# Source lists of a sparse graph network: which operand of the list products moves

## The chip, the cores and the metric

The kernel runs on one core of a Trainium2 chip. The time is that of the device for one execution, in microseconds, as the median of several runs. Beside these runs there is one profiled execution, from which all durations come. The engines are TensorE (PE, with its weight loads as PEld), VectorE (DVE), ScalarE (ACT), GpSimd (POOL) and SyncE (SP, a queue of DMAs).

## The reference

Four graph attention layers run one after the other over 4096 nodes of 256 features, all with the same 0/1 adjacency matrix of 4096 x 4096 (about one entry in 256 is set, many more for the first nodes than for the last). Each layer normalises its input, applies ReLU, and adds its attention to the input:

```python
h = jnp.maximum(_layernorm(x, axis=-1), 0.0)
x = x + layer(h, adj, ...)
# in a layer, in short:
h = x @ W
e = leaky_relu((h @ a1)[:, None] + (h @ a2)[None, :])
attn = softmax(where(adj > 0, e, NEG), axis=1)
out = attn @ h            # layer 2 has 4 heads, layer 3 a positive and a negative softmax
```

## The kernel before

**Dense blocks and listed tiles.** Targets are handled in 8 blocks of 512 or in 32 row tiles of 128. The first blocks of each layer are dense (4 in layer 0, then 2, 1, 1): all 32 source tiles are weighed and multiplied. For the other row tiles the sources beyond the first 512 nodes are listed. Since few sources have an edge into a tile, each tile T has CAPS[T] columns (5 to 12) of 128 source numbers each. A column serves either one quarter of the tile's 32 targets (a quad is four such columns) or the whole tile. GpSimd gathers feature rows by these numbers with indirect DMAs (L532).

**How a list is made.** The lists are made once, during layer 0, by `list_sources(ib, ...)` for the blocks 1 to 7, 28 row tiles in all. VectorE finds from the mask which sources each quarter sees. Two products with triangular and all-ones matrices, `pre` (L864) and `tot` (L866), and a scan give every used source a place. The place is split in a column number (`hib`) and a row within the column (`lof`). `val` holds for each column the source's number where it belongs to that column, and else 0. `one_hot` (L943) makes `first[p, i, j]`, which is 1 where source p of source tile j has row i; one such tile is for 14 of the 28 source tiles, and j is its innermost index, so the 128 entries of one j lie 28 bytes apart. Then, for each row tile, 28 products, one for each source tile j, add up the list (L968): the one-hot is the weights, and val moves, CAPS[T] columns of it. The result is `idx_ps`, 128 rows by CAPS[T] columns; VectorE adds an offset and writes it as the integers `idx` (L978), which the gathers read.

**The order of work.** `run(plan)` writes out by hand the order in which instructions are issued. A step of the plan is one source tile of one unit (a dense block or a listed tile). Each step goes through fetch, begin, weigh (on VectorE, `s_p`, L1151, or L1110 for quads) and multiply (on TensorE, `s_acc`, L1193, or L1130 for quads, whose products are 32 columns wide), which come 0, 2, 3 and 6 steps after one another. After each multiply, `pump` gives turns to waiting generators: `posts` (ends of units and the next layer's projections, `s_tp`, L746, `s_hT`, L748, and `s_pj`, L778) and `lists_q` (the list being made). A turn runs to the generator's next `yield`. The first dense blocks and listed tiles give the list two turns a step, dense block 2 three and dense block 3 four. When layer 0's plan is over, lists and posts are drained with one turn each in alternation; layer 1 follows.

**What is shared.** TensorE, VectorE and ScalarE each work in the order of issue. The PSUM pool `ps_mm` has two buffers under the tag "mm", for the list's results and sums, `s_tp`, `s_pj` and the target rows `s_sT` (L1036). The list's `idx_ps` holds one of them from a tile's first product to `idx`. ScalarE, besides copies and exponentials, copies masks out of gathered rows (L1084, L1174), and waits for those gathers.

Of the kernel before, what the change touches and what calls it, by code (L numbers as in the profile page):

```python
# [8 lines left out]
F32 = mybir.dt.float32  # L9
F16 = mybir.dt.float16  # L10
# [4 lines left out]
ALU = mybir.AluOpType  # L15
# [3 lines left out]
P = 128  # L19
# [438 lines left out]
JT = NT - DP  # L458
# [5 lines left out]
GR = 4  # L464
GP = P // GR
# [3 lines left out]
MAXCAP = max(CAPS)  # L469
# [20 lines left out]
def list_layers(ctx: ExitStack, tc: tile.TileContext, a: dict, out: bass.AP, flag):  # L490

    nc = tc.nc

    const = ctx.enter_context(tc.tile_pool(name="s_const", bufs=1))
# [6 lines left out]
    ps_mm = ctx.enter_context(tc.tile_pool(name="s_mm", bufs=2, space=PSUM))  # L501
# [11 lines left out]
    onesb = const.tile([P, P], F16, name="s_onesb")  # L513
# [3 lines left out]
        tri, onesb, pattern=[[1, P]], compare_op=ALU.is_gt, fill=0.0, base=0, channel_multiplier=-1  # L517
    )
    nc.gpsimd.affine_select(
        tri, tri, pattern=[[1, P]], compare_op=ALU.not_equal, fill=-float(BASE), base=0, channel_multiplier=-1  # L520
    )
    places = const.tile([P, NT - TS0], F32, name="places")
    for T in range(TS0, NT):
        nc.gpsimd.memset(places[:, T - TS0 : T - TS0 + 1], float(2 * BASE + P * SHARED[T]))
# [326 lines left out]
    def list_sources(ib, seen, pool, consts):  # L851
# [3 lines left out]
        half = JT // 2  # L855
        quads = QUADS[ib * IT]
        cap = max(CAPS[ib * IT : (ib + 1) * IT])
# [68 lines left out]
        val = pool.tile([P, MAXCAP, n], F16, name=f"val_{ib}", tag="val")  # L926
# [13 lines left out]
        def one_hot(T, j):  # L940

            first = pool.tile([P, P, half], F16, name=f"first_{T}_{j}", tag="first", bufs=2)
            nc.vector.tensor_tensor(  # L943
                first,
                place,
                lof[:, T % IT, j : j + half].unsqueeze(1).to_broadcast([P, P, half]),
                op=ALU.is_equal,
            )
            return first
# [5 lines left out]
        for t in range(IT):  # L955
            T = ib * IT + t
            cap = CAPS[T]
            ps = None
            for j in range(JT):
                if j % half == 0:  # L960
                    first = firsts.pop()
                    ahead.pop(0)
                    if ahead:
                        firsts.append(one_hot(*ahead[0]))
                    yield
                if ps is None:
                    ps = ps_mm.tile([P, MAXCAP], F32, name=f"idx_ps_{T}", tag="mm")
                nc.tensor.matmul(  # L968
                    ps[:, 0:cap],
                    lhsT=first[:, :, j % half],  # L970
                    rhs=val[:, 0:cap, t * JT + j],
                    start=(j == 0),
                    stop=(j == JT - 1),
                )
                if j % 7 == 6:
                    yield
            idx = keep.tile([P, cap], I32, name=f"idx_{T}", tag=f"idx_{T}")
            nc.vector.tensor_scalar(idx, ps[:, 0:cap], float(HALF), None, op0=ALU.add)  # L978
            index[T] = idx
            yield  # L980
# [413 lines left out]
    with ExitStack() as phase:  # L1394
# [33 lines left out]
        half = CH // 2  # L1428
# [32 lines left out]
        def mask_chunk(ib, c):  # L1461
# [17 lines left out]
            if ib > 0:  # L1479
                if c == 0:  # L1480
                    seen[ib] = lists_p.tile([P, IT * GR, JT], BF16, name=f"seen_{ib}", tag="seen", bufs=4)
                else:
                    nc.vector.tensor_reduce(
                        seen[ib][:, :, (c - 1) * CH : c * CH].rearrange("p a j -> p j a"),
                        m.rearrange("p j i -> p (j i)")
                        .bitcast(I32)
                        .rearrange("p (j a w) -> p j a w", j=CH, w=GP // 4),
                        AX.X,
                        ALU.max,
                    )  # L1490
                if c == NCH - 1:
                    waiting[ib] = list_sources(ib, seen[ib], lists_p, consts)
                    while turns and turns[0] in waiting:
                        push(lists_q, waiting.pop(turns.pop(0)))
# [86 lines left out]
    for l in (1, 2, 3):  # L1581
# [37 lines left out]
        if l == 3:  # L1619
            one = Unit(L, 0, IT, NT, all_sources(L, 0, IT, [0], 1), big="growb", heads=[0])  # L1620
            two = Unit(L, 0, IT, NT, all_sources(L, 0, IT, [1], 1), big="growb", heads=[1], like=one)
            first = one.plan() + two.plan()
        else:
            per = L.H
            first = []
# [40 lines left out]
def gat_layers(tc: tile.TileContext, a: dict, out: bass.AP):  # L1666
    nc = tc.nc
    with tc.tile_pool(name="flag", bufs=1) as pool:
        flag = pool.tile([1, 1], I32, name="flag")

        with tc.manual_schedule(engines={mybir.EngineType.Pool}):
            list_layers(tc, a, out, flag)
        again = nc.values_load(flag[0:1, 0:1], min_val=0, max_val=1)
        with tc.If(again > 0):
            dense_layers(tc, a, out)
# [45 lines left out]
```

## Time and profile before

| | us |
|---|---|
| median of 3 runs | 1661.9 |
| their range | 1661.72 to 1684.04 |
| profiled execution | 1527.76 |
| its span | 1526.0 |

| in the profiled execution | |
|---|---|
| list products (L968) | 784, from 126.4 to 498.3 us |
| one-hots (L943) | 56 on VectorE, 1080 ns each |
| idx (L978) | 28, the first at 139.2, the last at 498.5 us |
| mean granted TensorE clock | 0.955 |

The page of a profile gives busy times, shares of the span and the chain of work that ended last. A product's duration includes the time that it needs to pass through the array, and products overlap, so what a product costs in a row of products is read from the distance of starts. "x <- y" after a wait means that x stood idle until y was done.

### The profile page before, as it was taken

The page shows a single profiled execution, that of the slowest core. Times are in us where ns is not written, and L with a number is a line of the kernel's source. Part 1 is how long each engine was busy: PE and PEld are TensorE (multiplying, and loading weights), DVE is VectorE, ACT ScalarE, POOL GpSimd, SP SyncE. Part 2 cuts the span into 40 slices and gives each one's busy share as a digit, 9 for nine tenths or more (in the row PEclk, how much of TensorE's full clock was granted, in tenths as well). Part 3 has the DMA queues.
Part 4 walks back from the last instruction along what each step waited for, and adds up shares of the span by engine and source line. Part 5 has one row for each costly group of instructions (what it writes and reads, how often), then busy time and mean ns, then how long its engine had stood idle before and what let it go on. Part 6 is the DMA issues. An engine that isn't in the chain of part 4 may idle for free.

```text
span 1526.0 us, 30153 instructions
## 1 busy us (share of the span) xinstructions
PE 1387.2 (91%) x10558; PEld 1051.8 (69%) x10558; DVE 1179.9 (77%) x3424; ACT 499.9 (33%) x1569; POOL 1061.1 (70%) x1255
## 2 busy tenths in 40 slices
PE   5999898989998999987898999999677999999995
PEld 4888676767776877775644655667565887878873
DVE  6979898999887478755598999999776466777764
ACT  5641012112112023332336666578662111111111
POOL 9832888888530578867608878888764588777775
PEclk9999999999998899999999999999888999999997
DMA  7899999997622455555514344345442677777665
GB/s 256 285 321 312 294 306 306 253 240 192 186 63 80 136 143 155 157 155 158 145 51 118 101 121 120 112 122 131 123 131 79 189 221 228 213 206 219 192 180 150
DMA packets 161024, 272.72 MB, mean 179 GB/s; under 512 B 29664, under 2 KB 86462, under 8 KB 160862
## 3 DMA queue, kind: packets, MB, share of 16 engines
q1 hardware_dynamic: 117322, 146.32, 30.8%
q0 software_dynamic: 42704, 123.84, 30.4%
q8 instruction: 86, 1.41, 0.4%
q14 instruction: 76, 0.62, 0.1%
q10 hardware_dynamic: 836, 0.53, 0.1%
HBM read 225.22 MB, written 45.39 MB: 177 GB/s over the span
## 4 chain that ended last, share of the span: by engine, by line
PE 52%; DVE 18%; DMA 11%; POOL 11%; issue 5%; ACT 2%; SPq 0%; POOLq 0%; DVEq 0%; ACTq 0%
PE s_acc L1193 31%; PE s_pj L778 8%; DVE s_p L1151 7%; POOL s_gq L532 5%; DMA s_gq<-table,idx 5%; DMA s_raw<-in_adjT 4%; PE s_acch L1210 3%; PE s_accm L1228 2%; PE s_acc L1130 2%; POOL s_gg L532 2%; DVE s_p L1160 2%; PE idx_ps L968 2%; PE s_tp L746 2%; POOL pause L541 1%; DVE s_m L1472 1%
## 5 line engine op out<-in xcount | busy, mean ns | idle before, releaser
L532 POOL DMA_INDIRECT s_gq<-table,idx x400 | 444.0, 1110 | 121.9 <-issue 83.1
L532 POOL DMA_INDIRECT s_gg<-table,idx x258 | 287.7, 1115 | 229.2 <-DVE bad L1015 58.5
L1193 PE MATMUL s_acc<-g,s_p 128*128 128x257 f32 x1152 | 294.8, 399 | 20.6 <-DVE s_p L1151 20.2
L1193 PEld LDWEIGHTS s_acc<-g,s_p 128*128 128x128 f32 x1152 | 219.0, 199 | 62.9 <-DVE s_p L1151 29.2
L1193 PE MATMUL s_acc<-s_gs,s_p 128*128 128x257 f32 x896 | 214.1, 390 | 0.0
L1151 DVE SCALAR_TENSOR_TENSOR s_p<-s_grow,pre,mpre 128x128 f32<-128x128 f32 (+1 forms) x576 | 188.4, 364 | 29.6 <-PE s_acc L1193 24.6
L778 PE MATMUL s_pj<-s_w,s_hT 128*128 128x259 f32 (+3 forms) x640 | 180.6, 421 | 17.5 <-ACT s_g L813 10.2
L1193 PEld LDWEIGHTS s_acc<-s_gs,s_p 128*128 128x128 f32 x896 | 167.9, 193 | 38.5 <-DVE s_p L1151 5.9
L1193 PE MATMUL s_acc<-pre,s_p 128*128 128x257 f32 x768 | 183.0, 386 | 2.3 <-DVE s_p L1151 1.5
L1151 DVE SCALAR_TENSOR_TENSOR s_p<-s_grow,s_gs,s_ms 128x512 f32<-128x512 f32 x224 | 157.7, 744 | 25.3 <-PE s_acc L1193 19.2
L1193 PEld LDWEIGHTS s_acc<-pre,s_p 128*128 128x128 f32 x768 | 145.0, 193 | 25.9 <-DVE s_p L1151 2.5
L778 PEld LDWEIGHTS s_pj<-s_w,s_hT 128*128 128x128 f32 x640 | 124.3, 205 | 48.1 <-ACT s_hT L748 11.4
L1193 PE MATMUL s_acc<-s_gg,s_p 128*128 128x257 f32 x530 | 136.0, 389 | 2.6 <-DVE s_p L1151 2.5
L532 POOL DMA_INDIRECT mlist<-mask_t,idx x77 | 89.3, 1160 | 65.5 <-DVE idx L978 46.7
L541 POOL MEMSET pause<- 128x256 f32 x379 | 132.6, 350 | 0.2
L1151 DVE SCALAR_TENSOR_TENSOR s_p<-s_grow,s_gg,mlist 128x128 f32<-128x128 f32 x363 | 116.3, 343 | 16.9 <-PE s_acc L1193 16.7
L1107 DVE TENSOR_TENSOR s_p<-s_grow,s_gq 128x128 f32<-128x128 f32 (+1 forms) x168 | 52.1, 337 | 96.5 <-DMA s_gq<-table,idx 61.6
L1042 ACT ACTIVATE s_grow<-s_sT 128x256 f32<-128x256 f32 (+2 forms) x136 | 46.9, 369 | 214.5 <-PE s_sT L1036 211.5
L1193 PEld LDWEIGHTS s_acc<-s_gg,s_p 128*128 128x128 f32 x530 | 100.6, 194 | 18.2 <-DVE s_p L1151 4.2
L1090 ACT ACTIVATE s_p<-s_grow,s_minus,pre 128x128 f32<-128x128 f32 x224 | 96.8, 486 | 39.5 <-PE s_accm L1228 19.6
L1228 PE MATMUL s_accm<-s_p,s_gs 128*65 128x512 f32 x224 | 102.6, 608 | 0.9 <-DVE s_p L1151 0.9
L1472 DVE TENSOR_SCALAR s_m<-s_raw 128x1024 uint8<-128x1024 int32 x112 | 85.6, 775 | 20.9 <-DMA s_raw<-in_adjT 20.7
(154 smaller groups left out, 1980.5 us busy)
## 6 DMA issues: line engine op xcount, KB each, us to landing
s_raw<-in_adjT SPq DMA_DIRECT2D x128, 512.0 KB
s_gs<-table SPq DMA_DIRECT2D x28, 516.0 KB
table<-s_g SPq DMA_DIRECT2D x28, 258.0 KB
mask_t<-s_m SPq DMA_DIRECT2D x28, 256.0 KB
s_ms<-mask_t SPq DMA_DIRECT2D x28, 256.0 KB
s_gq<-table,idx POOLq DMA_INDIRECT x400
table<-s_m SPq DMA_DIRECT2D x21, 256.0 KB
table<-g SPq DMA_DIRECT2D x8, 516.0 KB
```

The lines of the kernel that those rows point to most:

```text
L532: nc.gpsimd.indirect_dma_start(out=dst, out_offset=None, in_=src, in_offset=bass.IndirectOffsetOnAxis(ap=index_ap, axis=0), element_offset ...
L541: nc.gpsimd.memset(pause, 0.0)
L746: nc.tensor.transpose(tp[:, c, :], zs[k][:, c * P : (c + 1) * P], ident)
L778: nc.tensor.matmul(ps, lhsT=hT[:, c, :], rhs=L.w[:, c, k * (D + 6) : k * (D + 6) + cols], start=(c == 0), stop=(c == 1),)
L1042: nc.scalar.activation(grow[:, h1:h2, :], ps[:, h1 - h0 : h2 - h0].rearrange("p h a b -> p h (a b)"), AF.Exp, scale=scale,)
L1090: nc.scalar.activation(w[:, h, :], u.grow[:, h, :], AF.Relu, scale=g[h][:, n - 1 : n], bias=minus)
L1107: nc.vector.tensor_tensor(p4[:, h0:h1], grow[:, h0:h1], c[:, h0:h1].to_broadcast([P, h1 - h0, GR, GP]), op=op)
L1151: nc.vector.scalar_tensor_tensor(p[:, k, :], u.grow[:, h, :], g[k][:, n - 1 : n], m, op0=ALU.min if L.l == 3 and h == 1 else ALU.max, op1= ...
L1193: nc.tensor.matmul(u.accs[it][h], lhsT=p[:, k, it * P : (it + 1) * P], rhs=g[k][:, 0:n], start=first, stop=last, skip_group_check=u.quads > 0,
L1210: nc.tensor.matmul(u.accs[0][c : c + P // 2, h, :], lhsT=p[:, h, c : c + P // 2], rhs=g[h][:, 0 : DH + 1], start=first and h == 0, stop=la ...
L1228: nc.tensor.matmul(u.accs[h], lhsT=g[k][:, 0 : DH + 1], rhs=p[:, k, :], start=first, stop=last, skip_group_check=True,)
L1472: nc.vector.tensor_scalar(m[:, h * half : (h + 1) * half, :], raw, 0.0, None, op0=ALU.is_gt)
```

## The change

In the list products the operands change places. The weights are now the source numbers, `val[:, 0:cap, ...]`, at most 12 columns. They go into one of four parts of 32 columns of the array, part j % 4, and write to the 32 PSUM partitions of that part. What moves is the one-hot, 128 columns. So the list of a tile comes out transposed and in four partial sums, `idx_q`, 128 by 128. Before them, a product of ones with a one-hot fills the whole of `idx_q` with finite numbers, so that the rows that no part writes can be read. ScalarE copies `idx_q` as f16 to `res`. A last product, with `res` as the weights and a 0/1 matrix `pick` moving, adds the four partial sums and transposes them, so that `idx_ps` is as before. `pick` is made once, on GpSimd, at the start. One more `yield` stands between the copy and the last product, so a tile takes one turn more.

```diff
@@ -519,6 +519,12 @@
+    pick = const.tile([P, MAXCAP], F16, name="pick")
+    nc.gpsimd.memset(pick, 0.0)
+    for k in range(GR):
+        nc.gpsimd.affine_select(
+            pick, pick, pattern=[[1, MAXCAP]], compare_op=ALU.not_equal, fill=1.0, base=GP * k, channel_multiplier=-1
+        )
@@ -964,16 +970,24 @@
                 if ps is None:
-                    ps = ps_mm.tile([P, MAXCAP], F32, name=f"idx_ps_{T}", tag="mm")
+                    ps = ps_mm.tile([P, P], F32, name=f"idx_q_{T}", tag="mm")
+                    nc.tensor.matmul(ps, lhsT=onesb, rhs=first[:, :, 0], start=True, stop=False, skip_group_check=True)
+                k = j % GR * GP
                 nc.tensor.matmul(
-                    ps[:, 0:cap],
-                    lhsT=first[:, :, j % half],
-                    rhs=val[:, 0:cap, t * JT + j],
-                    start=(j == 0),
-                    stop=(j == JT - 1),
+                    ps[k : k + cap, :],
+                    lhsT=val[:, 0:cap, t * JT + j],
+                    rhs=first[:, :, j % half],
+                    start=(j < GR),
+                    stop=(j >= JT - GR),
+                    skip_group_check=True,
                 )
                 if j % 7 == 6:
                     yield
+            res = pool.tile([P, P], F16, name=f"idx_r_{T}", tag="idx_r")
+            nc.scalar.copy(res, ps)
+            yield
+            ps = ps_mm.tile([P, MAXCAP], F32, name=f"idx_ps_{T}", tag="mm")
+            nc.tensor.matmul(ps[:, 0:cap], lhsT=res, rhs=pick[:, 0:cap], start=True, stop=True)
             idx = keep.tile([P, cap], I32, name=f"idx_{T}", tag=f"idx_{T}")
             nc.vector.tensor_scalar(idx, ps[:, 0:cap], float(HALF), None, op0=ALU.add)
```

`GR` is 4, `GP` 32, `JT` 28, `half` 14 and `MAXCAP` 12.

## Prediction

> **What bounds the kernel now.** I began with the page, for the whole, and then the busy times of the stretch in which the lists are made (120 to 500 us), because the change touches nothing outside it.
>
> ```profile
> span 1526.0 us, 30153 instructions
> PE 1387.2 (91%) x10558; PEld 1051.8 (69%) x10558; DVE 1179.9 (77%) x3424; ACT 499.9 (33%) x1569; POOL 1061.1 (70%) x1255
> ```
> ```profile
> core 0: us, PE busy (x) PEld busy (x) DVE busy (x) ACT busy (x) POOL busy (x), PEclk, DMA share, GB/s
> 120.00:350.00 230.00, 206.30 (x1203) 167.23 (x1204) 207.34 (x504) 30.30 (x109) 178.08 (x196) 0.94 0.98 283
> 350.00:500.00 150.00, 137.41 (x923) 110.05 (x921) 123.05 (x349) 30.09 (x113) 63.64 (x73) 0.91 0.44 123
> ```
>
> Up to 350 us TensorE and VectorE are both at 90% and the DMA engines at 0.98: three resources near their limits. From 350 on the DMA share is 0.44 and TensorE leads with 92%. ScalarE is at 13 to 20%. Time taken from TensorE is thus worth something late and little early. The chain of waits cut to 120 to 500 us puts a number on it; its piece from 450 to 468 us shows the pattern.
>
> ```profile
> by line: PE s_acc L1193 20.6%; DMA s_raw<-in_adjT 14.8%; issue 7.6%; PE idx_ps L968 6.2%; PE s_pj L778 5.0%; DVE s_m L1472 4.8%; POOL s_gq L532 4.5%; DVE s_p L1151 4.2%; DMA table<-s_g 2.3%; DMA s_gq<-table,idx 2.1%; DMA mlist<-mask_t,idx 1
> ```
> ```profile
> 450.86 0.81 PE idx_ps L968 x14
> 451.66 0.57 PE s_acc L1130 x8
> 452.23 0.94 PE idx_ps L968 x14
> 453.17 2.27 PE s_acc L1193 x10
> ```
>
> The list products (L968) hold 6.2% of 380 us, 23.6 us. One run of 14 takes 0.81 us, 57 ns each; 784 of them are 44.7 us. So 23.6 / 44.7 = 0.53 of the time of the list products lies on the path. That is the rate at which I turn a change in their TensorE time into a change of the end.
>
> Next, what the products cost and what each new form would. These are rows of the views of the tiles concerned and of single lines (ns, least/median/most):
>
> ```profile
> L968 PEld LDWEIGHTS <-first x784: 137/159/194, 126.2 to 498.2; 128*128 128x128 f16 x196
> L968 PE MATMUL idx_ps<-val,first x784: 171/203/229, 126.4 to 498.3; 128*128 128x6 f16 x70, 128*128 128x7 f16 x42, 128*128 128x8 f16 x35, 128*128 128x10 f16 x14
> L866 PEld LDWEIGHTS <-s_onesb x14: 96/98/99, 95.4 to 479.1; 128*128 128x128 f16 x14
> L866 PE MATMUL tot_p<-pure,s_onesb x7: 356/359/359, 95.6 to 472.9; 128*128 128x464 f16 x7
> L866 PE MATMUL tot_s<-shared,s_onesb x7: 212/214/214, 110.1 to 479.1; 128*128 128x116 f16 x7
> ```
>
> Two things are to be seen. L866 gives the price of a moving column in f16: (359 - 214) / (464 - 116) = 0.42 ns, so 128 columns are 53 ns. And a load of 128 f16 columns takes 97 ns when they lie side by side (s_onesb) but at least 137 when they are 28 bytes apart (first[:, :, j]): the stride costs 40 ns for 128 elements.
>
> The timeline of TensorE shows 32-column parts in use already (L1130, the quads):
>
> ```profile
> 199.30 1.46 PE L1193 MATMUL s_acc<-g,s_p 128*128 128x257 f32 x6
> 200.69 0.64 PE L1130 MATMUL s_acc<-s_gq,s_p 128*32 128x257 f32 x8
> 201.26 1.57 PE L1193 MATMUL s_acc<-g,s_p 128*128 128x257 f32 x6
> ```
>
> Eight narrow products hold TensorE for 201.26 - 200.69 = 0.57 us. Eight wide ones of the same 257 columns take 8 x 217 ns = 1.74 us. So four parts do work side by side: two groups of four are 0.43 us of the 0.57, and most of the rest is the way back to the full array. Single starts show it: two wide products begin 0.217 us apart, but a wide and a narrow one 0.31 us, at the way in as at the way out. Each change of shape costs 0.09 us, 0.19 us per run.
>
> **What the Trainium skill says.** "TensorEngine Tiling (Array Packing)", section Key Properties: tiles work independently, but a change of the tiling mode drains TensorE. The trace agrees, with the 0.09 us above. The same page, section Restrictions, says that column tiling turns Fast Weight Load off; the lists' loads shrink from 128 columns to at most 12, so it matters little, and no row here shows it for f16. "SBUF — State Buffer", section Door 1, in its remark on cachelines: lines have 16 bytes, two hits per line are needed for full bandwidth, so 8 bf16 may be strided for free and a read that meets a new line each time pays. The 137 ns against 97 agree for weights. For a moving operand with that stride no row shows it, and this is the change's open question. "ScalarE: Activation LUTs", section What ACT_TABLE_LOAD costs, prices an ACTIVATE by a fixed part and 0.83 ns per column; I use the trace's 128x128 PSUM read at L1042, 276 ns.
>
> **The change, part by part.**
>
> (1) The 784 products. What moves is now the one-hot, 128 columns 28 bytes apart, four parts side by side. Bounds for a full group of four: 57 ns if the stride is free (53 and some issue), 107 ns if each column costs double, about 190 ns if reading lines is what counts. The last follows from the load: 128 lines cost 40 ns more than the 7 or so that contiguous ones need, some 47 ns; four streams of 128 lines are 190 ns if they share that rate. If instead every stream is slowed, 40 ns over the 32 columns of each of the load's four chunks is 1.25 ns on top of 0.42 per column, 213 ns. Both readings meet near 190, and I take that: 47 ns per product, 784 x 47 = 36.8 us.
>
> (2) Changes of shape. In TensorE's order the 784 products lie in 62 unbroken runs (36 of 14, 19 of 7, 7 others); each is entered from 128-column work and left to it: 62 x 0.19 = 11.5 us.
>
> (3) Added per row tile of 128 targets, 28 times: the product of ones (one-hot moving, 0.05 us) and the 0/1 product (a load of 128 and up to 12 columns, as L968 is now, 0.06 us): 3.1 us.
>
> TensorE's sum: 36.8 + 11.5 + 3.1 = 51.4 against 44.7, 6.7 us more. On the path, 0.53 of it: +3.5 us.
>
> (4) A new wait. The 0/1 product waits for ScalarE's copy, which waits for the last list product. Alone this is 0.20 (the product's end) + 0.28 (copy) + two hand-overs of 0.04 (idx starts 38 ns after its product in the trace) = 0.56 us. Behind it in TensorE's queue stand the next step's projections and s_acc products, and VectorE's idx (L978) waits for it, with s_p and first behind that. A step of 2 to 8 products (0.4 to 1.7 us) covers it where the pump gives two turns per step. It is bare where three or four turns fall together (dense blocks 2 and 3) and in the drained end after 480 us. I take 10 of 28 tiles: 5.6 us, about half on the path, +3 us. If all are covered it is 0, if none, 15.7. VectorE already waits there:
>
> ```profile
> DVE idx L978 <- PE idx_ps L968: 15.0, 12, 3.7
> ```
>
> Those 12 waits lengthen by the same 0.56 us, in the same places, so I don't count them again.
>
> (5) Nothing elsewhere. Four affine_selects and a memset on GpSimd before 10 us, beside an iota of 4.6 us: below 1 us, hidden by the wait for s_raw. 28 copies of 0.28 us on ScalarE, 7.8 us on an engine at 16%. One more turn per tile delays a list by 4 turns of about 47: the queue has gaps (no list product from 225 to 275 us), so only the last lists feel it. No DMA is issued or moved; SP's and POOL's orders stay, and gathers follow idx. One PSUM buffer more is taken for a short time from the two of "mm"; it is free once the copy has read.
>
> Sum: +3.5 + 3 = +6.5 us. Against the profiled execution: 1527.8 + 6.5 = 1534.3 us. The median of the timed runs is 1661.9, 134 us above the profiled execution, and nothing in the page says why; I add the same difference: 1668 us. About 2% (33 us) is what a measurement of this kernel can tell from no change, so I expect no visible change.
>
> **Rivals.**
>
> Free stride (0.32). The 62 runs make 221 groups of up to four; at 57 ns that is 12.6 us, with 11.5 and 3.1 27.2 us, so 17.5 us less on TensorE. 0.53 of it is 9.3; with (4) 6 us are left: 1656 us. If all of it were on the path, 1661.9 - 17.5 = 1644. For it: the contiguous quads run at full rate in four parts. Against: 137 against 97 ns.
>
> A slow hand-over (0.08), on the other side. The 0/1 product stands in order behind ScalarE, and ScalarE sometimes stands still for a gather:
>
> ```profile
> ACT mlist L1084 <- DMA s_gq<-table_own,idx: 18.3, 4, 5.5
> ACT mlist L1174 <- DMA s_gg<-table_own,idx: 15.4, 7, 5.1
> ```
>
> If the copy of a list is queued behind such a wait, TensorE stops for up to 5.5 us with everything behind it. It decides from a mean of 33 / 28 = 1.2 us per tile, wholly on the path; at 1.3 us it gives +36, 1698 us. Against: these waits lie between 400 and 442 us, where only 4 of the 28 tiles end, and the step's own product waits for the same gather.
>
> No parallel streams (0.05): the parts take turns at 57 ns. Then the products save nothing and 14.6 us are added: 7.7 on the path, with (4) 11 us, 1673 us. L1130 speaks against it.
>
> **How the numbers follow.** The forecast has 0.50, the free stride 0.32, the slow hand-over 0.08, turns 0.05, and 0.05 is for a gain above 2%, for which list time and the waits it causes on VectorE would both have to go. Hence faster 0.05, same 0.87, slower 0.08. The three runs span 22 us, and the open costs run from -17.5 to +36. The range 1640 to 1695 holds forecast, free stride and turns with that scatter and most of the rest.
>
> **What would show it.** Right: the moved one-hots' products about 47 ns apart on average in a full run, a run of 14 near 0.85 us, the share of list products on the path unchanged, and TensorE waiting some 0.5 us for the copy in about ten tiles. A run of 14 at 0.4 us would show the free stride. Waits of over 1 us for the copy in most tiles would show the slow hand-over. The forecast is wrong if the time leaves 1640 to 1695.

## The result, and the profile after

The changed kernel takes 1670.2 us (median of 20 runs), the kernel before 1661.6 (20 runs). By these medians it is slower by 8.6 us where 6.5 were forecast (1668), inside the range and inside the 2% that were called no change. The ratio that was computed is larger, 1.011 with an interval of 1.0068 to 1.0153, because it leaves out, for each kernel, the runs more than 1.5% above its fastest, which are 12 of the kernel before and 4 of the changed one. Over all runs the medians give 1.005 and the means 1.006.

The runs come in sets of two kinds: in kind A (chips 14 and 15 on record) both kernels take about 1525 us, as in the profiled execution before, and in kind B (chip 5 where the record names one) about 1640 to 1670, as in the timed runs and in the profile after, so ratios are used only within one set and times of profiles are compared only within one kind. Repeated in a set of kind A, the changed kernel is at 1.0044 (1.0021 to 1.0067), or +6.7 us.

These are lines of the profile after, taken in a set of kind B: the page, the busy times of two stretches (the second ends with the lists), and the chain of waits from 120 to 500 us.

```profile
span 1677.2 us, 30298 instructions
PE 1476.8 (88%) x10614; PEld 1057.9 (63%) x10614; DVE 1178.9 (70%) x3424; ACT 503.9 (30%) x1597; POOL 1037.5 (62%) x1260
```
```profile
120.00:350.00 230.00, 199.37 (x1115) 136.99 (x1114) 186.25 (x451) 29.05 (x108) 162.89 (x182) 0.93 0.87 264
350.00:540.00 190.00, 169.49 (x1065) 109.18 (x1064) 143.03 (x410) 37.67 (x141) 75.52 (x87) 0.92 0.43 123
```
```profile
by line: PE s_acc L1207 37.9%; another core or an unknown queue 12.8%; PE idx_q L976 9.6%; PE s_pj L784 5.3%; DVE s_m L1486 4.4%; DVE s_p L1165 4.3%; issue 4.2%; DMA s_gg<-table,idx 2.2%; DVE seen L1497 1.9%; PE s_acc L1144 1.6%; PE s_tp L7
```

The "unknown queue" holds 12.8% of this stretch and nothing in any profile of a set of kind A, the changed kernel's included. It also shows in every profile of a set of kind B, so it goes with the condition. How much of it falls into this stretch differs from profile to profile (7.0% in a variant of the kernel before, next to nothing in two others), and there is no profile of the kernel before in kind B; so it is not shown that the change adds nothing to it. What belongs to the change is seen in the list products: within kind A, L976 has 8.8% of this chain (r1_after) where L968 has 5.7% (r0_before). The rows of these products and two pieces of the chain say why.

```profile
L976 PEld LDWEIGHTS <-val x784: 86/95/118, 128.8 to 539.1; 128*6 128x6 f16 x70, 128*7 128x7 f16 x42, 128*8 128x8 f16 x35, 128*10 128x10 f16 x14
L976 PE MATMUL idx_q<-first,val x784: 387/409/429, 128.8 to 539.4; 128*6 128x128 f16 x70, 128*7 128x128 f16 x42, 128*8 128x128 f16 x35, 128*10 128x128 f16 x14
```
```profile
493.37 1.01 PE idx_q L976 x14
496.56 0.56 PE idx_q L976 x7
```

A run of 14 now takes 1.01 us on the path; it was 0.81. A product lasts 409 ns though only 128 columns move. Single starts in the trace come in fours, mostly 1 to 8 ns apart, and the next four begin about 224 ns later. So the parts do work side by side, but each moving column costs 224 / 128 = 1.75 ns, not 0.42.

### The profile page after: what moved, and what is told of

The parts are those of the page before. It is cut to its first block, busy times and chain, and to the rows that moved or that the text cites. A ratio compares the mean times of both kernels' runs of the same rounds, so it can differ in the third digit from the quotient of the medians.

```text
span 1677.2 us, 30298 instructions
## 1 busy us (share of the span) xinstructions
PE 1476.8 (88%) x10614; PEld 1057.9 (63%) x10614; DVE 1178.9 (70%) x3424; ACT 503.9 (30%) x1597; POOL 1037.5 (62%) x1260
## 4 chain that ended last, share of the span: by engine, by line
PE 70%; DVE 10%; issue 6%; POOL 5%; another core or an unknown queue 4%; DMA 2%; ACT 2%; DVEq 0%; POOLq 0%; ACTq 0%
PE s_acc L1207 37%; PE s_pj L784 9%; PE s_acch L1224 7%; PE s_accm L1242 6%; DVE s_p L1165 3%; PE idx_q L976 3%; PE s_acc L1144 3%; PE s_sT L1050 2%; POOL s_gq L538 2%; PE s_tp L752 2%; PE s_acch L1144 1%; DVE s_m L1486 1%; DMA s_gq<-table,idx 1%; DMA s_gg<-table,idx 1%
## 5 line engine op out<-in xcount | busy, mean ns | idle before, releaser
L538 POOL DMA_INDIRECT s_gq<-table,idx x400 | 426.8, 1067 | 193.5 <-issue 82.6
L538 POOL DMA_INDIRECT s_gg<-table,idx x258 | 284.3, 1102 | 308.4 <-PE idx_ps L990 61.0
L1207 PE MATMUL s_acc<-s_gs,s_p 128*128 128x257 f32 x896 | 218.4, 395 | 3.3 <-issue 2.1
L784 PE MATMUL s_pj<-s_w,s_hT 128*128 128x259 f32 (+3 forms) x640 | 191.2, 440 | 21.3 <-issue 8.8
L1207 PEld LDWEIGHTS s_acc<-s_gs,s_p 128*128 128x128 f32 x896 | 170.2, 196 | 43.8 <-issue 12.7
L784 PEld LDWEIGHTS s_pj<-s_w,s_hT 128*128 128x128 f32 x640 | 129.4, 214 | 56.4 <-issue 13.3
L547 POOL MEMSET pause<- 128x256 f32 x379 | 128.4, 339 | 0.2
L1224 PE MATMUL s_acch<-pre,s_p 128*64 128x65 f32 x1792 | 91.5, 238 | 24.3 <-issue 22.3
L1224 PEld LDWEIGHTS s_acch<-pre,s_p 128*64 128x64 f32 x1792 | 71.6, 145 | 61.4 <-issue 35.5
```

The costliest lines, as they stand in the source:

```text
L538: nc.gpsimd.indirect_dma_start(out=dst, out_offset=None, in_=src, in_offset=bass.IndirectOffsetOnAxis(ap=index_ap, axis=0), element_offset ...
L547: nc.gpsimd.memset(pause, 0.0)
L784: nc.tensor.matmul(ps, lhsT=hT[:, c, :], rhs=L.w[:, c, k * (D + 6) : k * (D + 6) + cols], start=(c == 0), stop=(c == 1),)
L1207: nc.tensor.matmul(u.accs[it][h], lhsT=p[:, k, it * P : (it + 1) * P], rhs=g[k][:, 0:n], start=first, stop=last, skip_group_check=u.quads > 0,
L1224: nc.tensor.matmul(u.accs[0][c : c + P // 2, h, :], lhsT=p[:, h, c : c + P // 2], rhs=g[h][:, 0 : DH + 1], start=first and h == 0, stop=la ...
```

## The experiments

In all of them "TensorE's time for the lists" is the sum, over the list products and those that the change adds, of the time from one start to the next start on TensorE. A start that comes later than 0.45 us counts as 0.45, so that waits are left out.

| kernel | set | TensorE for lists, us | last idx starts at, us | ratio to before (95%) |
|---|---|---|---|---|
| before (first profile; e0_before; r0_before) | A | 48.7; 48.2; 48.6 | 498.5; 504.7; 498.3 | 1 |
| changed (r1_after) | A | 67.4 | 502.2 | 1.0044 (1.0021 to 1.0067) |
| before, more products (r3_more) | A | 67.4 | 508.8 | 1.0083 (1.0054 to 1.0111) |
| changed, pairs (e1_pairs) | A | 32.3 | 498.6 | 1.0014 (0.9994 to 1.0033) |
| before, pairs (r2_before_pairs) | A | 25.8 | 498.2 | 0.9984 (0.9962 to 1.0006) |
| changed, flat (e2_flat) | A | 35.9 | 533.8 | 1.027 (1.0227 to 1.0314) |
| changed, delayed (e6_cover) | A | 69.7 | 525.2 | 1.0173 (1.0134 to 1.0212) |
| changed (result) | B | 69.1 | 540.4 | 1.011 (1.0068 to 1.0153) |
| changed (e9_after) | B | 67.5 | 531.0 | 1.0225 (1.0147 to 1.0304) |
| before, more products (e10_more) | B | 68.4 | 543.2 | 1.0217 (1.0124 to 1.0311) |
| before, pairs (e4_before_pairs) | B | 26.3 | 505.0 | 1.0175 (1.0091 to 1.0258) |
| changed, pairs, bare (e5_pairs_bare) | B | 32.4 | 503.3 | 1.0104 (0.9999 to 1.0209) |

The three profiles of the kernel before show what single profiles scatter by: their last idx starts up to 6 us apart. The last four rows share a set in which the runs of before lay between 1609 and 1652 us; their ratios are all raised by the lowest of these. Their medians (six runs each) are 1655.9, 1660.4, 1645.5 and 1639.8 beside 1642.7 of before, and only their order is used.

**The kernel before again.** No edit.

> The kernel before, unaltered, for a second profile of it. Its first profiled execution took 1527.8 us, while the 20 timed runs lie between 1636 and 1684. If that execution was an odd one, this profile shows a span near 1660, with list products (L968) again 60 ns apart and the additional time in stretches that the change does not touch. If profiles of this kernel are always that fast, it shows about 1527.

It took 1529.2 us, with a span of 1527.5, in a set where 27 runs of before have a median of 1525.8. So the first profile was no odd execution: times near 1527 are what this kernel takes in a set of kind A.

**One-hots in pairs.** The entries of two source tiles lie side by side, so the moving operand steps by 4 bytes. These are the main lines; the `iota` that fills `place` and the product of ones follow suit:

```diff
-        place = pool.tile([P, P, JT // 2], F16, name="place")
+        place = pool.tile([P, JT // 4, P, 2], F16, name="place")
-            first = pool.tile([P, P, half], F16, ...)
+            first = pool.tile([P, half // 2, P, 2], F16, ...)
-                lof[:, T % IT, j : j + half].unsqueeze(1).to_broadcast([P, P, half]),
+                lof[:, T % IT, j : j + half].rearrange("p (a b) -> p a b", b=2).unsqueeze(2).to_broadcast([P, half // 2, P, 2]),
-                    rhs=first[:, :, j % half],
+                    rhs=first[:, j % half // 2, :, j % 2],
```

> The changed kernel with the one-hots of two source tiles side by side, so that what moves has steps of 4 bytes in place of 28. Theory (stride): what moves is slowed[...], 224 ns per group of four as the profile after shows; four entries per line bring a group to 57 to 110 ns, a run of 14 from 1.02 us (start to next start) to 0.4 to 0.65, some 25 us less on TensorE over all lists, about half of it on the path: 1.011 of before falls to about 1.00. Rival (hand-over): the loss is the wait for ScalarE's copy; products get shorter but the time stays at 1.011. Rival (VectorE): the new layout costs VectorE its double speed, one-hots go from 1.08 to 1.9 us and the time rises by up to 45 us.

Rows of the one-hots' tile in this kernel, then a run of 14 with its neighbours in TensorE's timeline:

```profile
L979 PE MATMUL idx_q<-first,val x784: 217/222/314, 132.7 to 497.8; 128*6 128x128 f16 x70, 128*7 128x128 f16 x42, 128*8 128x128 f16 x35, 128*10 128x128 f16 x14
L949 DVE TENSOR_TENSOR first<-place,lof x56: 1056/1083/1093, 123.2 to 496.4; 128x1792 f16<-128x1792 f16 x56
L977 PE MATMUL idx_q<-first,s_onesb x28: 217/220/314, 132.5 to 496.5; 128*128 128x128 f16 x28
```
```profile
470.33 0.41 PE L979 MATMUL idx_q<-first,val 128*8 128x128 f16 x14
470.53 0.59 PE L1147 MATMUL s_acc<-s_gq,s_p 128*32 128x257 f32 x2
```

The product falls from 409 to 222 ns, and the 14 products are through in 0.20 us, when the next quad begins. VectorE keeps its speed. TensorE's time for the lists is half of the changed kernel's. The theory of the stride is confirmed for the product, and the other rival fails, since one-hots keep their speed. The time comes to 1.0014, level with before, as expected; but TensorE spends 16 us less than before on the lists, and none of it is seen in the time.

**One-hots flat.** All 128 entries side by side, `first` as [P, half, P], with `lof` repeated along the innermost axis.

> The changed kernel with the 128 entries of each one-hot side by side. Theory (stride): a group of four takes about 57 ns, a run of 14 about 0.40 us; but VectorE's in1 repeats one element, so its one-hots should fall to single speed, 1.08 to about 1.9 us, 45 us more on VectorE over 56 of them, which is 87% busy there: time 1.00 to 1.025 of before. Rival (hand-over): products shorter and the rest as in the changed kernel, at 1.011 and more. If the group stays near 224 ns, the stride is not what slows it.

```profile
L976 PE MATMUL idx_q<-first,val x784: 216/219/314, 128.2 to 532.8; 128*6 128x128 f16 x70, 128*7 128x128 f16 x42, 128*8 128x128 f16 x35, 128*10 128x128 f16 x14
L949 DVE TENSOR_TENSOR first<-place,lof x56: 1990/2015/2078, 117.2 to 530.5; 128x1792 f16<-128x1792 f16 x56
```

The products gain next to nothing over pairs (219 against 222 ns): a step of 4 bytes is small enough. The one-hots take 2.02 us in place of 1.08, 52 us more on VectorE, and the end comes 38 us (medians) to 41 us (ratio) later, slightly more than expected: VectorE's time counts at 0.7 to 0.8 of itself in this stage.

**The hand-over delayed.** `yield` after the copy becomes `yield 2.0`.

> The changed kernel with 2 us of the plan's clock between ScalarE's copy and the 0/1 product (two dense steps or five listed ones), so that other products stand before the waiting one. Theory (stride): TensorE's waits for the copy (42.7 us in 16 times in the profile after, 23 of them in one odd stop) fall to under 10, but the products keep 224 ns per group, and the time stays within 5 us of the changed kernel, 1.008 to 1.012 of before. Rival (hand-over): the loss goes with the waits, to 1.00.

Neither expectation of the time held: 1.0173. What TensorE waits for ahead of the 0/1 product, in this kernel and in the changed one (r1_after), and below it the two parts of the latter:

```profile
  ACT idx_r L987: 8.7, 15
```
```profile
  ACT idx_r L987: 8.9, 15
```
```profile
  PEld L990: 6.4, 8
  PE idx_ps L990: 2.6, 7
```

The total counts most stops twice, at the load and again at the product. By single starts it is 7 of 28 tiles in which the load stands 0.7 to 0.95 us and the product comes about 0.6 us later than it would. The delay did not shrink these waits, and the last list is ready at 525 us, not at 502. By the order of work, a tile's delay pushes all later turns of its list back. So the kernel is sensitive to when a list is ready, and a delay is a poor way to cover a hand-over.

**More products, no other change.** In the kernel before, 12 products more at the start of each tile, which the real ones overwrite; TensorE's time for the lists becomes that of the changed kernel.

```diff
+                for _ in range(12 if j == 0 else 0):
+                    nc.tensor.matmul(ps[:, 0:cap], lhsT=first[:, :, j % half], rhs=val[:, 0:cap, t * JT + j], start=True, stop=True)
```

> The kernel before with 12 more list products at the start of each tile, overwritten by the real ones: 28 x 12 x 60 ns = 20 us more on TensorE, without moving one-hots, without parts of the array, without a hand-over. Theory (TensorE time alone makes the loss, at nearly full rate): ratio 1.010 to 1.014. If only 0.53 of such time reaches the end, as predicted: 1.007. Rival (hand-over, or changes of the array's shape): 1.000 to 1.003.

> The kernel before with 20 us of additional list products on TensorE again, for a narrower interval. If the loss of the change is TensorE's time alone: 1.010 to 1.015, like the changed kernel, and the last idx 15 to 35 us late. If it were the hand-over or the changes of shape: 1.000 to 1.003.

With 67.4 us for the lists, as much as the changed kernel, and without moved one-hots, parts of the array or a copy, it is at 1.0083 in the set of kind A, between the rate of 0.53 and the full rate; its last idx is 10 us late, less than expected. In the set of kind B it is 4.5 us behind the changed kernel by medians. More time on TensorE in this stage is thus enough to make a loss of this size, and a larger one than the change itself makes in kind A.

**The changed kernel beside its variants.**

> The changed kernel, unaltered, beside its own variants and the kernel before, since the chip of the earlier runs was some 135 us slower with both kernels. Theory (TensorE time): the list products hold TensorE 20 us longer than before, with the product of ones and the 0/1 product 28 us, so the ratio lies between 1.011 and 1.018 here too, like the variant with a covered hand-over (1.0173). Rival (the other chip[...] made the loss): here the ratio is under 1.006.

> The changed kernel again, because the runs of before scattered by 2.6% in its last comparison and its interval (1.0147 to 1.0304) is too wide. Theory: TensorE holds the lists 20 to 28 us longer, nearly all of it reaches the end: 1.012 to 1.019, last idx at 525 to 540 us. Rival (only 0.53 of it reaches the end): 1.007 to 1.009.

In the set of kind B its median is 13 us above that of before; in the set of kind A it is at 1.0044, below both expectations. The view by stretches of r0_before, then of r1_after, then of r3_more, all of the same set of kind A:

```profile
120.00:350.00 230.00, 205.18 (x1193) 165.16 (x1193) 205.78 (x497) 30.22 (x109) 180.05 (x194) 0.95 0.94 281
350.00:498.00 148.00, 134.65 (x925) 109.00 (x924) 124.03 (x355) 29.90 (x112) 62.34 (x72) 0.93 0.43 126
```
```profile
120.00:350.00 230.00, 213.43 (x1242) 149.05 (x1242) 209.93 (x517) 33.71 (x124) 179.32 (x199) 0.98 0.95 288
350.00:502.00 152.00, 140.42 (x933) 90.87 (x931) 118.85 (x335) 32.97 (x125) 58.95 (x69) 0.97 0.39 114
```
```profile
120.00:350.00 230.00, 212.66 (x1341) 172.76 (x1342) 205.11 (x499) 30.10 (x109) 179.91 (x193) 0.96 0.93 281
350.00:509.00 159.00, 149.99 (x1116) 123.30 (x1115) 124.01 (x355) 29.79 (x112) 63.16 (x76) 0.90 0.41 119
```

TensorE is busy 8 us longer in the first stretch and 6 us in the second, which is 4 us longer; these are differences between single profiles, and the 4 us lie within their scatter.

One column sets the changed kernel apart from the other two. The third number from the end is the share of its full clock that TensorE was granted: 0.95 and 0.93 before, 0.98 and 0.97 in the changed kernel, 0.96 and 0.90 with more products. Each stretch times its missing share gives an estimate of what TensorE lost to a reduced clock: 22 us before (23 and 27 in its other two profiles), 9 in the changed kernel, 25 in r3_more. The wide `s_acc` products, which no variant alters, show it too: in the list stage they start 240 ns apart on average before, 241 in r3_more and 232 in the changed kernel. It is no chance of one profile: in this set the mean clock of a whole execution is 0.963 to 0.970 in 15 runs of the changed kernel, 0.950 to 0.963 in 32 of before and 0.951 to 0.961 in 10 of r3_more.

**Pairs in the kernel before.** Only the layout of the one-hots, which are the weights there.

> The kernel before with the one-hots of two source tiles side by side, which are its weights: steps of 4 bytes in place of 28, and nothing else. Theory (stride): the load of 128 columns takes about 97 to 110 ns in place of 137 to 159, products follow each other every 30 to 50 ns in place of 60, and the lists hold TensorE 8 to 20 us less. If a gain on TensorE is worth 0.53 of itself, 0.992 to 0.997 of before. If the list stage is bound elsewhere (VectorE, gathers) once TensorE has room, as the changed kernel with pairs suggests, 1.000 within its interval. If the changed kernel with pairs stayed at 1.001 only because its hand-over ate the gain, this one, which has none, is at 0.99 or below.

> The kernel before with paired one-hots again (products 25 ns apart in place of 60, the lists 20 us shorter on TensorE), for a narrower interval. If time taken from TensorE in this stage were worth 0.53 of itself: 0.993. If the stage is held by VectorE and the gathers once TensorE has room: 0.998 to 1.003, last idx near 500 us as before.

The rows of the tile in r2_before_pairs, and its timeline:

```profile
L971 PEld LDWEIGHTS <-first x784: 96/97/153, 131.3 to 497.9; 128*128 128x128 f16 x196
L971 PE MATMUL idx_ps<-val,first x784: 169/175/217, 131.5 to 498.0; 128*128 128x6 f16 x70, 128*128 128x7 f16 x42, 128*128 128x8 f16 x35, 128*128 128x10 f16 x14
```
```profile
455.71 0.53 PE L971 MATMUL idx_ps<-val,first 128*128 128x9 f16 x14
456.16 0.64 PE L1133 MATMUL s_acc<-s_gq,s_p 128*32 128x257 f32 x8
```

The load falls to the 97 ns of a contiguous one, and products come 26 ns apart in place of 60: TensorE's time for the lists is cut by 22.8 us, more than in any variant of the change, without a hand-over. The last idx still comes at 498 us, and 0.9984 cannot be told from 1. It has the lowest ratio of all kernels in sets of kind A, but it is not shown to beat the kernel before.

**Pairs with a bare hand-over.** The pairs variant without the added `yield`.

> The changed kernel with paired one-hots and without the yield between ScalarE's copy and the 0/1 product, so that nothing covers the hand-over in any tile. Theory: each tile stops TensorE some 0.45 us (6 us in 14 waits become about 12 in 28), at most +6 us on 1526: 1.001 to 1.005. Rival (hand-over is what costs): clearly slower than the variant with the yield (1.0014), 1.010 or more.

TensorE's loads of `res` wait 6.2 us for the copy in 9 tiles, where those of the pairs variant wait 4.1 in 9. The median is 2.9 us below that of before. The interval, up to 1.0209, excludes little; but nothing points to a large cost. In the same set the changed kernel has a median 16 us higher. That agrees with a loss from the stride, but the profiles differ also in the "unknown queue", which holds much more of the changed kernel's list stage.

## Why the prediction was right, and where its terms were off

The direction, the range and "no visible change" held, and so did the main reason: a moving one-hot with a step of 28 bytes gives back what four parallel parts gain. That is shown by the pairs, which alone take TensorE's time for the lists from 67.4 to 32.3 us. How near the number came is luck, as the terms show. Of the signs named, the waits for the copy came about as described; but a run of 14 takes 1.02 us to the next start, not 0.85, and the products' share of the path rose. By steps:

- **Step (1), the products.** Of the two readings that met near 190 ns per group, the second is right: every stream is slowed by itself. The group takes 224 ns, beyond the 213 worked out for it. A lone stream shows it: the product of ones takes 391 ns at 28 bytes (line below) and 220 in pairs. With the changes of shape I had 36.8 + 11.5 = 48.3 us; the trace has 56.5.
- **Step (2), changes of shape.** The way in (310 ns from a wide product's start in place of 217) and the way out are about as priced, some 0.2 us per run. The trace before has 61 runs, not 62, which changes nothing.
- **Step (3), added products.** This failed most in proportion. I took 0.05 us for the product of ones, as if its stride were free, against my own step (1), and added no change of shape after it. It holds TensorE 0.32 us, 9.1 us in all, where 1.4 were counted. The 0/1 product was right (1.8 us against 1.7).
- **TensorE's sum** was to rise by 6.7 us, from 44.7 to 51.4, and rose by 18.8, from 48.6 to 67.4. Steps (1) and (2) miss 8 us and step (3) another 8; the start was set 4 us too low.
- **The rate of 0.53.** The number that the chain gave is not a constant. In the set of kind A, 18.8 us more gave about +12.7 us in r3_more (0.67) and, with 6 us of waits at loads besides, +6.7 in the changed kernel (0.36). 22.8 us less gave 2.4 (0.1), and 5.8 at the end of the interval (0.25). In sets of kind B the medians give 8.6 and 13 us for the changed kernel and 18 for e10_more, with runs of before that spread over more than 40 us.
- **A term at nothing: the clock.** The prediction lets the granted clock stay as it is. It rose in the changed kernel, worth an estimated 13 us of TensorE's time in the list stage of r1_after, and did not in r3_more. That fits the gap between their losses. It is not shown to be its cause: no run held the clock fixed, and why moved one-hots are granted more is open. The rise is smaller elsewhere: a mean of 0.959 in e6_cover (0.956 before) and 0.941 in e9_after (0.935 before), and none in the list stage of the profile after (0.93 and 0.92).
- **The forecast** thus met the +6.7 of a set of kind A, and the 8.6 of the medians in the result, because errors cancelled: a sum that was 12 us too small, a rate too large for what came of it, and a clock that was left out.
- **Step (4), the hand-over.** 10 bare tiles at 0.56 us were forecast, 5.6 us; in r1_after there are 7, whose products come about 0.6 us late, some 4 us. VectorE's waits for the indices were to lengthen by 0.56 us in 12 places, 6.7 us in all; they lengthened by 14 against r0_before (by 9 against e0_before, 19.9 us in 13) and became more. Here r0_before, then r1_after, and then the lone stream of step (1), in r1_after:

```profile
DVE idx L978 <- PE idx_ps L968: 14.8, 12, 4.5
```
```profile
DVE idx L992 <- PE idx_ps L990: 28.7, 18, 4.4
```
```profile
L974 PE MATMUL idx_q<-first,s_onesb x28: 387/391/414, 126.9 to 499.2; 128*128 128x128 f16 x28
```

- **The free stride and the slow hand-over**, the two main rivals, are refuted in kind A, the first by 224 ns per group, the second by waits of under 1 us in 7 tiles. In the profile after, of kind B, the loads wait 23 us for copies; 18 of these are two stops of 12 and 6 us, the longer behind a copy that itself stood behind the "unknown queue". So there the hand-over did cost more, in a way that the forecast named only for gathers. The parts do not take turns: four start within some 10 ns.

Where a gain would have gone is not shown. With pairs in either kernel the last list is ready at 498 us, where the kernel before has 498 to 505, though TensorE has 16 to 23 us less to do. In the chain of r2_before_pairs, s_acc has 14.9% (18.5% in r0_before) and the gathers (L532, s_gq) 9.4% (6.9%); but the three profiles of before scatter from 4.5 to 11.4% in that line, so this proves nothing. That VectorE and the gathers hold the stage once TensorE has room fits e2_flat, where VectorE's time counted at 0.7 to 0.8. A part of the gain may have gone into the clock: its mean is 0.953 in 14 runs of r2_before_pairs and 0.956 before, an estimated 5 us over the whole execution. None of these was taken apart. Open as well is what the losses in sets of kind B are made of.

## What to carry to other kernels

Before swapping the operands of a product, look at the step of what will move: the layout that VectorE found convenient cost TensorE fourfold per moving column here (224 ns in place of about 57 for four products), and two entries of 2 bytes side by side were enough to cure it, for weights and for moving data alike, at no cost to VectorE. Ask next whether the stage has room for the gain: a chain's share gave a rough price for losing time on an engine near its limit, and said little of what freeing it is worth. In this stage 19 us more on TensorE cost 7 to 13 us, and 23 us less gained at most 6. And look at the granted clock of both kernels before a difference in time is put down to an engine's work.

## What the hardware showed unexpectedly

- A moving f16 operand with a step of 28 bytes costs 1.75 ns per column (224 ns per 128), also for a single stream; with 4 bytes, as flat, a group of four takes 56 to 62 ns.
- Weights with that step: products 60 ns apart, 26 ns with a step of 4 bytes (loads 159 and 97 ns).
- VectorE's compare of 1792 f16 keeps 1.08 us when the repeated operand has runs of two different entries, and takes 2.02 us when one entry is repeated along the innermost axis.
- Within one set the granted clock differed with the kernel: with the same time on the lists (67.4 us) it was 0.98 and 0.97 in the two stretches of the list stage with moved one-hots, and 0.96 and 0.90 with more products of the old form.
